# Two expert layers on one core: fetching answers in two parts, moving a branch, and roots written as powers

## The chip, the cores and the metric

The kernel runs on one core of a Trainium2 chip. A core has a matrix engine (TensorE, PE in the profile, with PEld for its weight loads), a vector engine (VectorE, DVE), a scalar engine (ScalarE, ACT), a general engine (GpSimd, POOL) and a sequencer that here only issues DMAs and branches (SyncE, SP). ACT, POOL and SP issue DMAs on their own queues. Each engine runs its instructions in order and waits on semaphores for the others.

The metric is the time of one execution on the device in microseconds (us), the median of several runs.

## The reference

The kernel computes two layers over 8 sequences of 100 tokens with 512 channels, all in float32. A context of 722 rows per sequence is attended to.

```python
x = x + cross_attention_0(layernorm(x), context)   # 16 heads of 32, causal: only the first 100 context rows count
x = x + experts_0(layernorm(x))                    # top 2 of 8 experts, 512 -> 2048 -> 512, exact gelu
x = x + cross_attention_1(layernorm(x), context)   # 16 heads of 64, keys and values of the tokens and of the 722 rows
x = x + experts_1(layernorm(x))                    # top 2 of 8 experts, 512 -> 1024 -> 512, silu gate, layernorm behind
```

In an expert layer each token goes to the two experts with the largest router logits, and its two answers are summed with softmax weights:

```python
logits = xf @ Wg.T + bg
tp, ti = top_k(softmax(logits), 2);  tp = tp / (sum(tp) + 1e-8)
x = x + tp[0] * expert[ti[0]](xf) + tp[1] * expert[ti[1]](xf)
```

Which of a token's two answers is added first makes no difference to the sum but for rounding. Each layernorm needs one over the root of a variance plus 1e-5, for every token; where two layernorms follow each other (the outer one and the block's own), the kernel takes both in one step.

## The kernel before

The 800 tokens lie in seven row tiles of 128 tokens (the last has 32). The work runs in stages, and the times below are those of the profiled execution.

- **First attention (0 to 200 us)** and its output, layernorm and router (200 to 242). `Route.group` sorts the tokens of some row tiles by expert and scatters their rows with indirect DMAs into a table `sent` in device memory (L274). `Route.order` ranks the experts by load: the fullest one gets slot 0, and so on. `values_load` (L304) brings the expert numbers of the slots into registers of SP and POOL, since they address the weights and the tables.
- **First experts (244 to 630).** `work_off` runs the eight slots one after the other. `arrived` (L351) loads a slot's rows and turns them into columns, `hidden0` does the first product (L695) with gelu on ACT, `products` the second (L363) with its bias on DVE, `returned` turns the result back and writes it with a POOL DMA (L384) to a table `answers`. The answers of slot k are written during slot k+1. Each slot has a fixed capacity (256 rows in slot 0, 176 in slot 7).
- **The branch (`rest`, L403 and L404).** If some expert has more tokens than its slot's capacity, a second round does the rest. The number `more` is loaded into registers of every engine, and every engine compares and branches. With these inputs the round is skipped. A branch also ends a block of instructions: the scheduler of the framework reorders the instructions of a block by priority and readiness, and moves none across the branch. In the kernel before it stands behind the experts.
- **Between the layers (630 to 685).** `project_early` computes five units of keys (L432, copied by ACT in L436) and values (transposes L444, copied by ACT in L446 to L449) of the second attention ahead of time. Then for each of the seven row tiles: `fetch` (L340) gathers the first answer and then the second of each token from `answers` with indirect DMAs on POOL, into a tile with two buffers; DVE adds each, scaled (L738); DVE takes mean and variance (L129, L131); `factors` makes one over the root, with ACT's Sqrt (L139) and DVE's reciprocal (L142), and the shift (L144); DVE scales (L148); PE turns the tile into columns (L159), and ACT writes these with gain and shift into `xT` (L168); POOL adds the output bias (L744). At the end the loads of the next weights start behind one-element POOL copies (L56), on SP's queue (L58).
- **Second attention (685 to 1490).** First the queries (L421). Then 64 units (sequence, pair of heads): scores (L793), row maximum on DVE (L797), exponential on ACT (L799), transposes (L822 to L828, copied by DVE and ACT), weighted values (L843). Whenever a row tile's units are done, `output` (L891) projects it, DVE adds it to x, and mean, variance and `factors` (ACT's Sqrt in L141) prepare it for the router; `logits1` (L175) and the scatter of `sent_on` follow one and two units later. Five row tiles come out inside the stage, near 924, 1015, 1139, 1328 and 1428 us, and two at its end. ACT holds the tables of one set of functions at a time: an ACT_TABLE_LOAD stands in the trace wherever an exponential follows a root or the reverse.
- **Second experts (1531 to 1831)**, another branch, and the final gathers, layernorm and output (to 1872).

The order on each engine is the framework scheduler's, block by block; DMAs are issued in the order of their queue. Weights come through a pool of eight 1 MB tiles, loaded by SP in the order of use; a load waits until the tile's last reader is done.

Of the kernel before, what the change touches and what calls it, by code (L numbers as in the profile page):

```python
# [66 lines left out]
def two_layers(ctx: ExitStack, tc: tile.TileContext, a: dict, out: bass.AP):  # L67
# [48 lines left out]
    nc.vector.memset(eps2, EPS * EPS)  # L116
    rank = const.tile([P, NE], F32, name="rank")
# [16 lines left out]
    def factors(mv, tag, twice=False):  # L134


        r = small.tile([P, 1], F32, tag=f"r{tag}", name=f"r{tag}")
        if twice:
            nc.scalar.activation(r, mv[:, 1:], AF.Sqrt, bias=eps2, scale=1.0 + EPS)  # L139
        else:  # L140
            nc.scalar.activation(r, mv[:, 1:], AF.Sqrt, bias=eps)  # L141
        nc.vector.reciprocal(r, r)  # L142
        t = small.tile([P, 1], F32, tag=f"t{tag}", name=f"t{tag}")
        nc.vector.scalar_tensor_tensor(t, mv[:, :1], -1.0, r, ALU.mult, ALU.mult)  # L144
        return r, t
# [61 lines left out]
    class Route:  # L207


        def __init__(self, layer, psum, tag):  # L210
# [6 lines left out]
            ]  # L217
            self.sel = routes.tile([P, NTILE, NE], F32, tag="sel", name=f"sel{layer}")
# [7 lines left out]
        def largest(self, v, m, name):  # L226
# [3 lines left out]
            at = self.temp([P, NTILE, NE], f"at{name}")[:, :g, :]  # L230
# [7 lines left out]
        def group(self, i0, i1, xn, held=()):  # L238
# [3 lines left out]
            at1 = self.largest(v, self.m[0][:, i0:i1], 1)  # L242
            other = self.temp([P, NTILE, NE], "other")[:, :g, :]
            nc.vector.scalar_tensor_tensor(other, at1, -3e38, v, ALU.mult, ALU.add)
            at2 = self.largest(other, self.m[1][:, i0:i1], 2)
# [17 lines left out]
            for k, at in enumerate((at1, at2)):  # L263
                pick = self.temp([P, NTILE, NE], "pick")[:, :g, :]
                nc.vector.tensor_tensor(pick, at, row, ALU.mult)
                place = self.temp([P, NTILE], "place")[:, :g]
                nc.vector.tensor_reduce(place, pick, AX.X, ALU.add)
                nc.vector.tensor_copy(self.where[k][:, i0:i1], place)
# [12 lines left out]
        def order(self, load):  # L281
# [7 lines left out]
            slot = self.temp([P, NE], "slot")  # L289
# [28 lines left out]
            nc.vector.tensor_copy(self.more, most)  # L318

# [66 lines left out]
    def work_off(jobs, arrive, hidden, product, send_back, first=None, midway=None):  # L386
# [5 lines left out]
        for k, (e, r0, n, w1, w2) in enumerate(jobs):  # L392
            h = hidden(e, n, x, w1, lambda: done and send_back(*done))
# [83 lines left out]
    with tc.tile_pool(name="a0", bufs=1) as ap, tc.tile_pool(name="a0w", bufs=3) as aw, tc.tile_pool(  # L477
# [193 lines left out]
        nc.vector.tensor_tensor(m2, m2, s, ALU.mult)  # L671


    with f0, tc.tile_pool(name="f0w", bufs=2) as fw, tc.tile_pool(
# [29 lines left out]
        def work0(jobs, first=None, midway=None):  # L704
# [3 lines left out]
                lambda e, r0, n, yT: returned(0, e, r0, n, yT, fp, ps), first, midway,  # L708
            )

        weights.limit = W_L1A + 4
# [6 lines left out]
        ], W_L0F, fetch_context)  # L718
        rest(
            more, work0, lambda piece, e, g: piece(of(0, "W1", e, g)), lambda piece, e, g: piece(of(0, "W2", e, g)), 4  # L720
        )

# [8 lines left out]
        xT1 = columns_tile("xT1")  # L731
        for i in range(NTILE):
            w = rows[i]
            both = fp.tile([P, 2, D], F32, tag="nil", name="back0", bufs=2)
            for k, m in enumerate((m1, m2)):
                y = both[:, k]
                fetch(y, where, i, k)
                nc.vector.scalar_tensor_tensor(  # L738
                    x[:w, i, :], y[:w], m[:w, i : i + 1], x[:w, i, :], ALU.mult, ALU.add
                )  # L740
            xn = fp.tile([P, D], F32, tag="mv", name="xn1", bufs=2)
            scaled(xn, x[:, i, :], *factors(moments(x[:, i, :], "a1"), "b", twice=True))
            to_columns(xT1, xn, i * P, rows[i], ps, gamma1, beta1)
            nc.gpsimd.tensor_tensor(x[:, i, :], x[:, i, :], bo, ALU.add)  # L744
        weights.limit = len(pieces)
        weights.load(W_L1A + 8, y[:1, :1])


    with tc.tile_pool(name="a1", bufs=1) as ap, ExitStack() as later, tc.tile_pool(
# [136 lines left out]
        def output(i):  # L886
# [9 lines left out]
            scaled(xn, x[:, i, :], *factors(moments(x[:, i, :], "f1"), "a"))  # L896
# [189 lines left out]
```

## Time and profile before

| | us |
|---|---|
| time before, median of 3 runs | 1872.75 (1872.5 to 1874.85) |
| profiled execution, its own time | 1873.61 |
| its span | 1872.1 |
| mean granted clock of PE | 0.962 of full speed |
| PE busy | 1730.2 (92%) |
| DVE busy | 593.0 (32%) |
| ACT busy | 482.6 (26%) |
| POOL busy | 151.6 (8%) |

The span runs from the first to the last instruction in the trace; the execution's own time is some 1.5 us longer. PE's busy share is a mean over stages. How it falls over the stages is read from windows of the trace, which give the busy time of every engine in a stretch, the clock that PE was granted there, and the share of time in which the DMA engines were busy. In a timeline of the trace each line is a group of like instructions: start, length, engine, line of the kernel, operation, what it writes and reads, and in brackets how long the engine had been idle before and which event ended that. In the list of waits a line says which tile an engine waited for, on whom, and then the sum of these waits, their number and the longest.

### The profile page before, as it was taken

The page shows a single profiled execution, that of the slowest core. Times are in us where ns is not written, and L with a number is a line of the kernel's source. Part 1 is how long each engine was busy: PE and PEld are TensorE (multiplying, and loading weights), DVE is VectorE, ACT ScalarE, POOL GpSimd, SP SyncE. Part 2 cuts the span into 40 slices and gives each one's busy share as a digit, 9 for nine tenths or more (in the row PEclk, how much of TensorE's full clock was granted, in tenths as well). Part 3 has the DMA queues.
Part 4 walks back from the last instruction along what each step waited for, and adds up shares of the span by engine and source line. Part 5 has one row for each costly group of instructions (what it writes and reads, how often), then busy time and mean ns, then how long its engine had stood idle before and what let it go on. Part 6 is the DMA issues. An engine that isn't in the chain of part 4 may idle for free. (4 is left out here: it accounts for less than half of the span.)

```text
span 1872.1 us, 26461 instructions
## 1 busy us (share of the span) xinstructions
PE 1730.2 (92%) x10422; PEld 1308.1 (70%) x10422; DVE 593.0 (32%) x1455; ACT 482.6 (26%) x1409; POOL 151.6 (8%) x245
## 2 busy tenths in 40 slices
PE   5999899999999879999999999999999839999990
PEld 2455579999999745666666666666666528999990
DVE  4464510111111130455444333444444331111115
ACT  2364321111111131333333323333333210010110
POOL 4010310000000130000000000000000030000003
PEclk9999999999999989999999999999999969999995
DMA  9911384465555371132010300211201145555513
GB/s 367 414 64 57 119 326 167 172 224 179 205 202 217 116 269 46 32 96 72 25 48 5 60 3 4 37 6 37 26 6 15 5 179 207 200 185 204 203 72 114
DMA packets 74982, 233.35 MB, mean 125 GB/s; under 512 B 23548, under 2 KB 35952, under 8 KB 58456
## 3 DMA queue, kind: packets, MB, share of 16 engines
q1 hardware_dynamic: 53348, 183.47, 28.4%
q0 software_dynamic: 9888, 30.06, 5.0%
q10 hardware_dynamic: 11604, 17.95, 3.1%
q8 instruction: 86, 1.41, 0.3%
q14 instruction: 56, 0.46, 0.1%
HBM read 180.41 MB, written 51.05 MB: 124 GB/s over the span
## 5 line engine op out<-in xcount | busy, mean ns | idle before, releaser
L432 PE MATMUL ps_m<-cb,w 128*128 128x361 f32 x896 | 302.4, 489 | 0.0
L363 PE MATMUL ps_y<-h,w 128*128 128x256 f32 (+7 forms) x1536 | 280.5, 344 | 0.0
L363 PEld LDWEIGHTS ps_y<-h,w 128*128 128x128 f32 x1536 | 268.6, 190 | 7.9
L432 PEld LDWEIGHTS ps_m<-cb,w 128*128 128x128 f32 x896 | 172.0, 197 | 103.7 <-issue 16.9
L695 PE MATMUL ps_h<-xgT,w 128*128 128x256 f32 (+7 forms) x1024 | 188.8, 345 | 0.0
L695 PEld LDWEIGHTS ps_h<-xgT,w 128*128 128x128 f32 x1024 | 180.3, 191 | 5.7 <-ACT h L699 0.2
L799 ACT ACTIVATE pr<-ps_sc,m 100x822 f32<-100x822 f32 x128 | 119.9, 942 | 176.2 <-DVE m L797 92.9
L797 DVE TENSOR_REDUCE m<-ps_sc 100x1 f32<-100x822 f32 x128 | 123.8, 1008 | 48.4 <-PE ps_sc L793 48.4
L823 DVE COPY prT<-ps_ptA 128x500 f32<-128x500 f32 x128 | 82.0, 678 | 178.2 <-PE ps_ptA L822 178.1
L699 ACT ACTIVATE h<-ps_h,s_b 128x256 f32<-128x256 f32 (+7 forms) x128 | 56.0, 438 | 303.6 <-PE ps_h L695 303.6
L436 ACT COPY mT<-ps_m 128x361 f32<-128x361 f32 x128 | 58.8, 460 | 254.7 <-PE ps_m L432 224.9
L421 PE MATMUL ps_col<-xT,w 128*128 128x400 f32 x320 | 115.0, 517 | 1.3 <-ACT xT L168 1.3
L965 PE MATMUL ps_g<-xgT,w 128*128 128x256 f32 (+7 forms) x512 | 104.0, 347 | 0.0
L965 PE MATMUL ps_u<-xgT,w 128*128 128x256 f32 (+7 forms) x512 | 102.8, 344 | 0.0
L421 PEld LDWEIGHTS ps_col<-xT,w 128*128 128x128 f32 x320 | 61.7, 196 | 47.4 <-issue 4.3
L965 PEld LDWEIGHTS ps_g<-xgT,w 128*128 128x128 f32 x512 | 91.2, 192 | 2.9
L793 PE MATMUL ps_sc<-mT,qT 64*100 64x411 f32 (+1 forms) x512 | 92.8, 468 | 0.0
L965 PEld LDWEIGHTS ps_u<-xgT,w 128*128 128x128 f32 x512 | 90.7, 190 | 2.6
L843 PEld LDWEIGHTS ps_av<-prT,mv 128*64 128x64 f32 (+1 forms) x1536 | 67.9, 137 | 27.2 <-issue 23.9
L970 ACT ACTIVATE sg<-ps_g 128x256 f32<-128x256 f32 (+7 forms) x64 | 22.3, 348 | 238.6 <-PE ps_g L965 238.6
L843 PE MATMUL ps_av<-prT,mv 128*64 128x100 f32 (+1 forms) x1536 | 80.6, 253 | 0.0
L822 PEld LDWEIGHTS ps_ptA<-ident,pr 100*128 100x128 f32 x640 | 65.3, 141 | 21.1 <-issue 11.0
(243 smaller groups left out, 1836.1 us busy)
## 6 DMA issues: line engine op xcount, KB each, us to landing
w<-in_W SPq DMA_DIRECT2D x64, 1024.0 KB
w<-in_w_gate SPq DMA_DIRECT2D x16, 1024.0 KB
w<-in_w_up SPq DMA_DIRECT2D x16, 1024.0 KB
w<-in_w_down SPq DMA_DIRECT2D x16, 1024.0 KB
sent<-nil SPq DMA_DIRECT2D x25, 512.0 KB
answers<-nil SPq DMA_DIRECT2D x25, 512.0 KB
cb<-in_ctxT ACTq DMA_DIRECT2D x16, 722.0 KB
mT<-kept_keys SPq DMA_DIRECT2D x13, 361.0 KB
```

The lines of the kernel that those rows point to most:

```text
L363: nc.tensor.matmul(py[:, k, :n], ws[f // 4][:, f % 4, dc * P : (dc + 1) * P], h[:, f, :n], start=f == 0, stop=f == nf - 1,)
L421: nc.tensor.matmul(ps[:, :HALF], w[c // 4][:, dc, (c % 4) * P : (c % 4 + 1) * P], xT[:, dc, cols], start=dc == 0, stop=dc == DC - 1,)
L432: nc.tensor.matmul(pm[:, : S // 2], w_m[ic // 4][:, dc, (ic % 4) * P : (ic % 4 + 1) * P], cb[h][:, dc, : S // 2], start=dc == 0, stop=dc = ...
L436: nc.scalar.copy(mT[:, h * (S // 2) : (h + 1) * (S // 2)], pm[:, : S // 2])
L695: nc.tensor.matmul(ph[:, :n], w[:, dc, j * P : (j + 1) * P], xg[:, dc, :n], start=dc == 0, stop=dc == DC - 1,)
L793: nc.tensor.matmul(sc[:, bank, c0:c1], qT[r, ic, q0 : q0 + T], keys_, start=True, stop=True)
L797: nc.vector.tensor_reduce(m, sc[:, :, :NKH], AX.XY, ALU.max, negate=True)
L799: nc.scalar.activation(pr.rearrange("p (a n) -> p a n", a=2), sc[:, :, :NKH], AF.Exp, bias=m, accum_out=sums[:, j : j + 1],)
L822: nc.tensor.transpose(pt[:, c, :], pr[:, T + c * P : T + (c + 1) * P], ident[:T, :T])
L823: nc.vector.tensor_copy(prT[:, : NSC - 1, :], pt)
L843: nc.tensor.matmul(po[r, 0, :], vj, prT[j][:w, c, :], start=c == 0, stop=c == NSC)
L965: nc.tensor.matmul(p_[:, :n], w_[:, dc, j * P : (j + 1) * P], xg[:, dc, :n], start=dc == 0, stop=dc == DC - 1,)
```

## The change

The diff has five parts, and `half` is a new constant tile of -0.5.

1. `rest` of the first layer moves from behind the first experts to the front of them.
2. `by_slot`, new, runs after the router: for every token it exchanges its two answers (their places in the table and their weights `m1`, `m2`) where needed, so that index 0 is the answer of the earlier slot. To that end the two one-hot choices (`at`) and the places are kept in tiles of their own. An answer of index 0 thus always comes from one of the slots 0 to 6.
3. `fetch_firsts` gathers the seven tiles of first answers while the last expert runs, behind the writing of the answers of slot 6 (`ahead` in `work_off`); they go into the buffer of `xT`, which is free then, and one into the buffer of `o_b1`. DVE adds them to x in a loop behind the experts, which the scheduler places ahead of the last expert's bias additions.
4. The second answers get one tile `seconds` with seven parts in the buffer of `h`, and their gathers are issued one after the other. The tiles `xn` have four buffers instead of two; every other row tile's columns are written by DVE instead of ACT (`vector`); the bias additions on POOL stand in a loop behind (the scheduler places them between the powers).
5. `factors(by_power=True)` makes one over the root with two POOL operations (an addition, or a multiplication and addition, and a power with exponent -0.5) in place of ACT's Sqrt and DVE's reciprocal: for the seven tiles between the layers, and for the seven outputs of the second attention. Other uses of `factors` stay.

```diff
-    def factors(mv, tag, twice=False):
+    def factors(mv, tag, twice=False, by_power=False):
         r = small.tile([P, 1], F32, tag=f"r{tag}", name=f"r{tag}")
-        if twice:
-            nc.scalar.activation(r, mv[:, 1:], AF.Sqrt, bias=eps2, scale=1.0 + EPS)
+        if by_power:
+            if twice:
+                nc.gpsimd.tensor_scalar(r, mv[:, 1:], 1.0 + EPS, EPS * EPS, ALU.mult, ALU.add)
+                nc.gpsimd.tensor_tensor(r, r, half, ALU.pow)
+            else:
+                nc.gpsimd.tensor_scalar(r, mv[:, 1:], EPS, None, ALU.add)
+                nc.gpsimd.tensor_tensor(r, r, half, ALU.pow)
         else:
-            nc.scalar.activation(r, mv[:, 1:], AF.Sqrt, bias=eps)
-        nc.vector.reciprocal(r, r)
+            ...
+            nc.vector.reciprocal(r, r)
...
+        def by_slot(self, behind):
+            wide = self.temp([P, NTILE, NE], "pick")
+            nc.gpsimd.tensor_copy(wide[:1, 0, :1], behind[:1, :1])
+            slots = [self.temp([P, NTILE], t) for t in ("key", "mine")]
+            for at, t in zip(self.at, slots):
+                nc.vector.tensor_tensor(wide, at, self.slot.unsqueeze(1).to_broadcast([P, NTILE, NE]), ALU.mult)
+                nc.vector.tensor_reduce(t, wide, AX.X, ALU.add)
+            swap = slots[0]
+            nc.vector.tensor_tensor(swap, slots[0], slots[1], ALU.is_gt)
+            for pair in (self.places, self.m):
+                d = slots[1]
+                nc.vector.tensor_tensor(d, pair[1], pair[0], ALU.subtract)
+                nc.vector.tensor_tensor(d, d, swap, ALU.mult)
+                other = self.temp([P, NTILE], "first")
+                nc.vector.tensor_tensor(other, pair[1], d, ALU.subtract)
+                nc.vector.tensor_tensor(pair[0], pair[0], d, ALU.add)
+                nc.vector.tensor_copy(pair[1], other)
+            for k in range(2):
+                nc.vector.tensor_copy(self.where[k], self.places[k])
...
-    def work_off(jobs, arrive, hidden, product, send_back, first=None, midway=None):
+    def work_off(jobs, arrive, hidden, product, send_back, first=None, midway=None, ahead=None):
...
-            h = hidden(e, n, x, w1, lambda: done and send_back(*done))
+            last = k + 1 == len(jobs)
+            h = hidden(e, n, x, w1, lambda: (done and send_back(*done), last and ahead and ahead()))
...
+        route.by_slot(where[1])
...
+        firsts = turned_x.tile([P, NTILE - 1, D], F32, tag="xT", name="firsts")
+        firsts = [firsts[:, i] for i in range(NTILE - 1)]
+        SHORT_AT = rows.index(min(rows))
+        firsts.insert(SHORT_AT, fp.tile([P, D], F32, tag="o_b1", name="first_short"))
+        def fetch_firsts():
+            for i in range(NTILE):
+                fetch(firsts[i], where, i, 0)
+        rest(more, work0, ...)
         weights.limit = W_L1A + 4
         work0([
             ...
-        ], W_L0F, fetch_context)
-        rest(more, work0, ...)
+        ], W_L0F, fetch_context, fetch_firsts)
+        for i, w in enumerate(rows):
+            nc.vector.scalar_tensor_tensor(
+                x[:w, i, :], firsts[i][:w], m1[:w, i : i + 1], x[:w, i, :], ALU.mult, ALU.add
+            )
...
+        seconds = fw.tile([P, NTILE, D], F32, tag="h", name="seconds", bufs=1)
+        for i in range(NTILE):
+            fetch(seconds[:, i], where, i, 1)
         for i in range(NTILE):
             w = rows[i]
-            both = fp.tile([P, 2, D], F32, tag="nil", name="back0", bufs=2)
-            for k, m in enumerate((m1, m2)):
-                y = both[:, k]
-                fetch(y, where, i, k)
-                nc.vector.scalar_tensor_tensor(
-                    x[:w, i, :], y[:w], m[:w, i : i + 1], x[:w, i, :], ALU.mult, ALU.add
-                )
-            xn = fp.tile([P, D], F32, tag="mv", name="xn1", bufs=2)
-            scaled(xn, x[:, i, :], *factors(moments(x[:, i, :], "a1"), "b", twice=True))
-            to_columns(xT1, xn, i * P, rows[i], ps, gamma1, beta1)
+            nc.vector.scalar_tensor_tensor(
+                x[:w, i, :], seconds[:w, i, :], m2[:w, i : i + 1], x[:w, i, :], ALU.mult, ALU.add
+            )
+            xn = fp.tile([P, D], F32, tag=("mv", "nil")[i % 2], name="xn1", bufs=2)
+            scaled(xn, x[:, i, :], *factors(moments(x[:, i, :], "a1"), "b", twice=True, by_power=True))
+            to_columns(xT1, xn, i * P, rows[i], ps, gamma1, beta1, vector=i % 2 == 1)
+        for i in range(NTILE):
             nc.gpsimd.tensor_tensor(x[:, i, :], x[:, i, :], bo, ALU.add)
         weights.limit = len(pieces)
-        weights.load(W_L1A + 8, y[:1, :1])
+        weights.load(W_L1A + 8, seconds[:1, NTILE - 1, :1])
...
-            scaled(xn, x[:, i, :], *factors(moments(x[:, i, :], "f1"), "a"))
+            scaled(xn, x[:, i, :], *factors(moments(x[:, i, :], "f1"), "a", by_power=True))
```

## The prediction

> **What bounds the kernel now.** I read the stages first (busy time of each engine in eight stretches), since one share of busy time hides them.
>
> ```profile
> 244.00:630.00 386.00, 384.65 (x2167) 372.20 (x2168) 40.59 (x108) 57.31 (x129) 16.95 (x36) 1.00 0.55 201
> 630.00:685.00 55.00, 37.95 (x149) 23.78 (x147) 26.71 (x53) 21.69 (x61) 25.15 (x27) 0.86 0.61 211
> 685.00:1490.00 805.00, 788.45 (x5157) 504.39 (x5158) 321.10 (x656) 265.17 (x734) 16.81 (x34) 0.98 0.17 36
> ```
>
> The columns are length, busy PE, PEld, DVE, ACT, POOL, granted clock, DMA share, GB/s. PE fills the first experts (384.65 of 386 us) and nearly fills the second attention (788.45 of 805). Only the stretch between the layers has idle PE worth a name, 17 us. So three places can answer the change: that stretch, PE's few pauses in the attention, and the start of the experts, where the branch goes.
>
> Between the layers I read the timeline of POOL, DVE, ACT and PE. Lines are start, length, engine, operation, and in brackets the idle time before and its releaser.
>
> ```profile
> 642.39 1.05 POOL L340 DMA_INDIRECT back<-answers,where  x1 [5.91 <-ACT mv L449]
> 664.57 1.14 POOL L340 DMA_INDIRECT back<-answers,where  x1 [0.30 <-issue]
> 646.81 1.54 DVE L738 SCALAR_TENSOR_TENSOR x<-back,m,x 128x512 f32<-128x512 f32 x2 [13.88 <-DMA back<-answers,where]
> 649.85 0.29 ACT L139 ACTIVATE rb<-mv_a,eps 128x1 f32<-128x1 f32 x1 [4.95 <-DVE mv_a L131]
> 678.42 0.16 DVE L142 RECIPROCAL rb<-rb 128x1 f32<-128x1 f32 x1 [5.15 <-ACT rb L139]
> 682.52 0.55 DVE L148 TENSOR_SCALAR xn<-x,rb,tb 128x512 f32<-128x512 f32 x1
> 685.09 5.61 PE L421 MATMUL ps_col<-xT,w 128*128 128x400 f32 x8 [1.27 <-ACT xT L168]
> ```
>
> Fourteen gathers run from 642.39 to 665.7; then ACT is the bottleneck: it does the root (L139) and the eviction (L168) in one queue, and DVE stands 5.15 us for a root. The last xn ends at 683.07, the projection starts at 685.09. PE's own waits there:
>
> ```profile
> PE ps_mv L444 <- ACT mT L436: 8.3, 5, 4.6
> PE ps_tp L159 <- DVE tb L144: 3.4, 1, 3.4
> ```
>
> The 4.6 is ACT standing at the root (649.85) with the keys' eviction behind it.
>
> In the attention I looked where an output tile (L891) is followed by its root, at the second of five places:
>
> ```profile
> 1013.78 1.28 ACT L799 ACT_TABLE_LOAD   x1 [3.01 <-issue]
> ...
> 1016.16 0.41 PE L793 MATMUL ps_sc<-kT,qT 64*100 64x100 f32 x2 [1.55 <-ACT pr L799]
> 1017.09 0.41 PE L793 MATMUL ps_sc<-kT,qT 64*100 64x100 f32 x2 [0.51 <-ACT pr L799]
> 1017.71 1.48 PE L175 MATMUL ps_lg<-p_w_router,xTf 128*128 128x8 f32 x8 [0.20 <-ACT xTf L161]
> 1019.04 8.05 PE L432 MATMUL ps_m<-cb,w 128*128 128x361 f32 x16
> ```
>
> The exponential reloads its table after the root, PE waits 2.06 us, and then 16 matmuls that elsewhere take 5.03 us take 8.05. The granted clock in short steps shows why (the first two steps are from the first layer's router, for comparison):
>
> ```profile
> 214.00:217.00 3.00, 1.56 (x12) 1.28 (x13) 2.49 (x18) 1.91 (x6) 0.00 (x0) 1.00 0.30 90
> 220.00:223.00 3.00, 0.56 (x1) 0.50 (x2) 2.65 (x22) 1.18 (x3) 1.91 (x2) 0.50 0.56 216
> ...
> 1015.00:1020.00 5.00, 3.12 (x14) 2.52 (x15) 1.06 (x6) 2.64 (x7) 0.00 (x0) 0.82 0.02 0
> 1020.00:1025.00 5.00, 5.00 (x9) 2.81 (x9) 1.91 (x12) 0.46 (x1) 0.00 (x0) 0.50 0.07 3
> 1025.00:1030.00 5.00, 5.00 (x35) 3.45 (x33) 2.36 (x5) 1.22 (x5) 0.00 (x0) 1.00 0.05 8
> ```
>
> **Attention (before 1490): roots as powers.** Two POOL operations replace ACT's root (0.29 us) and DVE's reciprocal (0.16) per output; with no root, both table loads per output go. Five outputs (around 924, 1015, 1139, 1328, 1428) lie inside the stage. PE's waits there are 1.33 + 4 x 2.06 = 9.6 us. Without the 1.28 us load before the exponential, each first wait (1.33 or 1.55) shrinks by that: 5 x 1.28 = 6.4 us. The clock: the following projection's matmuls cost 2.6, 3.0, 2.4, 1.8 and 1.5 us more than at full clock (0.314 us each), 11.3; the router's eight tiny matmuls before them up to 0.8 more than their 1.06, 2.2 in sum: 13.5 us. Does the clock come back with the waits? In the first layer's router, with the same tiny matmuls but pauses of at most 1.05 us, the clock holds 1.00; the pause of 3.11 us at 219.3 to 222.4 halves it. 0.27 + 0.51 us would remain, nearer to the first case, so I let four of five falls go: 10.8. Sum -17; ends -6.4 (only waits) and -20. The cover for the power: mv_f is ready at 914.26 and DVE's next copy that PE needs (prT, behind the scaling in DVE's queue) starts at 917.92, so 3.7 us are free. ACT loses work here and nobody waits for it more.
>
> The skill ("TensorE: Matmul & The Clock Gate", Part 1) says the gate halves the clock after at least one idle window of about 3.4 us. Taken strictly, pauses of 2.06 us would not halve it, the fall would have another cause, and the attention's gain would be 6.4, the sum about 1857. The trace shows the clock at 0.50 right behind such a pause, so I keep the rows' figure.
>
> **Price of the power.** No such operation is in the trace. Nearest POOL rows: a 1x1 copy 0.17, a 100x128 copy 0.29, a 128x512 addition 1.26. The operand is 128x1, so I take 0.3 for each of the two operations, ends 0.17 and 1.26.
>
> **Between the layers.** First answers: seven gathers (0.97 us + 0.30 issue, from the rows above 1.27 each) go behind expert 6's answers, which landed at 603.89 and 608.53. So they run from about 609 to 618, with x += of 7 x 0.75 us on DVE to about 623. The bias evictions of the last expert stand behind them on DVE; the first product pair is done at 620.8 and the other PSUM half is free, so PE waits for nothing. Cover gone: at most 2 us.
>
> Second answers start when the last expert's answers have landed (640.92 before). The branch was not their bound on POOL: its reset step waited for that same landing. So about 642, and with no buffer to wait for, 7 x 1.27 to 650.9. DVE sees the first one at about 646 (landing took 4.4 us in the first row). Then per tile x += 0.75, statistics 0.69 + 0.17, t 0.15, scaling 0.53: 2.29, seven tiles 16.0; four DVE evictions of tile 1 at 0.33 in between, 1.3; five of POOL's bias additions collide (one such collision stretched two x += from 1.5 to 3.08, so 0.75 each), 3.75; the last tile's trip to POOL behind one bias addition, about 2. The last xn ends at 646 + 16.0 + 1.3 + 3.75 + 2 = 669; eight DVE evictions of 0.33 and an ACT eviction follow, the projection starts at about 672.5 to 673. Against 685.09 that is -12. PE's early keys no longer bind: five units at 5.51 (the unstalled period at 231 to 236) from 630.6 to 661 after losing their stop behind the root. Ends: if the branch's absence on DVE lets the last answers be written 2.7 us earlier (POOL waited "[2.78 <-DVEq L404]" at 635.95), and the power is cheapest, -16. If each POOL operation costs 1.26, POOL does 7 x 2.5 + five additions of 1.26 + 0.5 of copies from 652 on, and ps_col starts at about 680: -5. The Wkv pieces come earlier; PE did not wait for them.
>
> **The branch in front.** After the layer PE lost nothing to it: its branch took 3.42 us at 631.84 while matmuls already queued ran on. In front PE has nothing queued. Last transposes end at 242.1, register load 0.75 (SP's row), branch 3.42: 246.3, against 244.44 for the first transposes of the gathered rows: +1.9. At ACT's and SP's 5.4 us for the branch, +3.8. If PE's branch is hidden after all, the rows' load remains: POOL's reset waits for the sends' landing (238.03, as the load's own wait does), then about 1.4 us to the next issue as at 641, where 0.7 stood: +0.8. I take +2. (The skill, "Advanced Engine Details and Errata", Control Flow Timing, prices a compare-and-branch at about 108 ns; by it the front would cost the +0.8 alone and the sum be about 1846. The branches of this trace took 2.9 to 5.4 us.) SP's seven weight loads move from 244.56 to some 250; the third piece is needed at 261.4: hidden, at most 5 us left of cover. DVE's by_slot (17 operations, 0.17 to 0.3 each, some 4 us) waits for the sends (238.03) to rewrite the places, then the branch of 2.9, to about 243, before the rows land at 244.3: hidden. The seven expert numbers loaded together on POOL (0.6 each) run in its wait of 10.0 us.
>
> **The last two outputs (1488, 1503)** lie on a bare chain: 0.45 us of root and reciprocal become two POOL operations, +0.15 each, with queue hops +0.25: +0.5; ends -0.2 and +4.
>
> **Sum.** -12 - 17 + 2 + 0.5 = -26.5 against the profiled execution's 1873.61 (span 1872.1 and 1.5 outside) gives 1847.1; the median of the three runs lies 0.86 below the profiled one, so 1846.2; I say 1847.
>
> **Rivals.** (A) Only the waits go, the clock falls as before, because the tiny matmuls after the output do it. For: it falls right at them. Against: the first layer's router. Attention -6.4 instead of -17: 1857. (B) The stretch between the layers is held by the answers' landing and by POOL's single queue, now with roots and additions: -5 there: 1853; together with A 1864. (C) The other side: the power is slow on POOL. With p us for a pair, the projection starts at 652 + 7p + 6.8 + 3.5; at p = 3.3 nothing is won between the layers, and from p = 3.7 each output also holds DVE's prT copy, and so PE. The total is 7(p - 3.3) + 5(p - 3.7) - 17 + 2.5; it turns slower at p = 4.7, and p = 6 gives +16: 1889. For: no row. Against: every POOL row of this size is under 0.3 us. (D) The change doesn't do what it says: the first gathers land too late, or x += waits on DVE into the last expert and holds its evictions. The landing at 608.53 and the 12 us to 620.8 speak against it; -4 in all there: 1854.
>
> **How the numbers follow.** Forecast 0.52, A 0.20, B 0.10, C 0.12, D 0.04, something near no change 0.02. Below 0.2% (3.7 us) a measurement of this kernel cannot tell from no change. Faster: forecast, A, B and D, less a little, 0.85; same 0.03; slower 0.12. The range runs from all good ends (-16 - 20 + 0.8 = -35.2: 1837) to A with B (1864). C stays out above it.
>
> **What would show it.** Right: no ACT_TABLE_LOAD and no wait over 0.6 us at the five outputs, 16 matmuls of L432 after them in about 5 us, first gathers before 620, the projection's first matmul some 42 us behind the end of the last product (630.2 before) instead of 55, the first ps_h 2 us later. Wrong: POOL rows of the power over 1.3 us; DVE idle "<-POOL r"; a clock of 0.5 at 1020 still; PE waiting for weights at the start of the experts; a branch of over 5 us on PE.

## The result and the profile after

The changed kernel takes 1858.86 us (median of 5 runs, 1856.08 to 1864.6) against 1874.85 us for the kernel before (5 runs): the ratio is 0.9921, with a 95% interval of 0.9896 to 0.9947. It is faster by 0.8%, about 16 us, where 26 had been forecast. The profiled execution is the slowest of the five (1864.6 us, span 1863.1); so the stages below say where time went, and the medians how much. All line numbers of the changed kernel differ from those of the kernel before (the products L695 are L732, the keys L432 are L468, the exponential L799 is L850, the gathers L340 are L375).

Cut at five marks of PE (end of the last value transposes before the experts, start of the first product, end of the last product, start of the projection, start of the last output's matmuls), the spans of the two profiles are, in us:

| stage | before | after |
|---|---|---|
| last transposes to first product of the experts | 5.3 | 11.6 |
| first experts, first to last product | 382.9 | 383.7 |
| last product to the projection | 54.8 | 45.3 |
| projection to the last output of the attention | 808.1 | 798.8 |
| the rest | 379.0 | 378.9 |

So the gain of 9.4 us between the layers and of 9.3 in the attention stands against a loss of 6.3 in front. (A further 2.7 us of this profile were lost earlier, in the router, where the clock fell 2.9 us sooner, at 216.59 instead of 219.45, around the same matmuls, and stayed low twice as long.)

The front, by the timeline of PE and POOL of the changed kernel (start, length, engine, operation, idle before and its releaser). The last line but one is PE's two branches (ns min/median/max, first and last start), and the last line is the same load in the kernel before:

```profile
244.11 0.66 PE L480 MATMUL ps_mv<-ident,mT 128*128 128x128 f32 x4 [0.33 <-ACT mT L472]
253.09 1.94 PE L169 MATMUL ps_tp<-ident,xg 128*128 128x128 f32 x8 [8.32 <-DMA xg<-sent]
256.38 5.89 PE L732 MATMUL ps_h<-xgT,w 128*128 128x256 f32 x16
249.40 1.18 POOL L386 DMA_DIRECT2D xg<-sent  x2 [15.74 <-PEq L440]
L440 PEldq COMPARE_BRANCH  x2: 3562/3915/4268, 244.7 to 1816.6; - x2
238.71 1.19 POOL L351 DMA_DIRECT2D xg<-sent  x2 [6.56 <-PE ps_m L432]
```

PE stands 8.32 us for the rows of the first expert. POOL had done its own part of the branch at 241.5, with the rows scattered (landed at 239.9); the load was issued at 249.40, and what released it is PE's sequencer at the branch (L440): PE's record of the branch lasts 4.27 us, to 249.0. The first rows landed at 252.95, and only then could PE transpose.

Between the layers (POOL, DVE, PE):

```profile
619.17 1.05 POOL L375 DMA_INDIRECT firsts<-answers,where  x1 [3.80 <-ACT h L736]
631.11 0.73 DVE L770 SCALAR_TENSOR_TENSOR x<-first_short,m,x 32x512 f32<-32x512 f32 x1
645.35 0.56 POOL L419 DMA_DIRECT2D answers<-y  x1 [2.39 <-DMA answers<-y]
648.41 1.01 POOL L375 DMA_INDIRECT seconds<-answers,where  x1 [2.50 <-ACT mv L485]
656.07 1.23 POOL L375 DMA_INDIRECT seconds<-answers,where  x1 [0.30 <-issue]
663.42 0.16 DVE L154 SCALAR_TENSOR_TENSOR tb<-mv_a,rb 128x1 f32<-128x1 f32 x1 [3.14 <-POOL rb L143]
679.03 0.55 DVE L158 TENSOR_SCALAR xn<-x,rb,tb 128x512 f32<-128x512 f32 x1
685.39 7.08 PE L457 MATMUL ps_col<-xT,w 128*128 128x400 f32 x12 [1.28 <-ACT xT L178]
```

Everything lies 9.7 us later than in the kernel before, since the experts ended at 640.08 instead of 630.34. The first answers are gathered and added under the last expert. The seven second gathers take 648.41 to 657.3; then the chain of DVE and POOL sets the end, with DVE idle for powers (the line at 663.42; in all 6.9 us over seven tiles).

The second attention at the same output as shown before:

```profile
1012.15 0.41 PE L844 MATMUL ps_sc<-kT,qT 64*100 64x100 f32 x2 [0.27 <-ACT pr L850]
1013.08 0.41 PE L844 MATMUL ps_sc<-kT,qT 64*100 64x100 f32 x2 [0.51 <-ACT pr L850]
1013.70 1.06 PE L185 MATMUL ps_lg<-p_w_router,xTf 128*128 128x8 f32 x8 [0.21 <-ACT xTf L171]
1014.61 6.80 PE L468 MATMUL ps_m<-cb,w 128*128 128x361 f32 x16
...
1423.58 5.11 PE L468 MATMUL ps_m<-cb,w 128*128 128x361 f32 x16
```

The wait of 1.55 us is 0.27, which is what the table load of 1.28 leaves. But the 16 matmuls behind still take 6.80 us here, 5.11 at the last of the five outputs. The windows of the trace (length, PE, PEld, DVE, ACT, POOL, clock, DMA share, GB/s) show the same two cases:

```profile
1010.00:1015.00 5.00, 4.01 (x46) 3.20 (x45) 2.46 (x6) 2.58 (x6) 0.00 (x0) 1.00 0.02 0
1015.00:1020.00 5.00, 5.00 (x12) 2.94 (x11) 2.40 (x14) 0.46 (x1) 0.00 (x0) 0.66 0.00 0
1418.00:1423.00 5.00, 4.01 (x45) 2.65 (x42) 2.56 (x6) 2.58 (x6) 0.00 (x0) 1.00 0.01 3
1423.00:1428.00 5.00, 5.00 (x22) 3.40 (x22) 2.31 (x14) 0.46 (x1) 0.00 (x0) 1.00 0.02 0
```

PE is busy for the same 4.01 of 5 us ahead of both, and once the clock falls (a mean of 0.66 over the next 5 us) and once it stays.

### The profile page after: what moved, and what is told of

It reads as the page before. It is cut to its first block, busy times and chain, and to the rows that moved or that the text cites. A ratio compares the mean times of both kernels' runs of the same rounds, so it can differ in the third digit from the quotient of the medians.

```text
span 1863.1 us, 26486 instructions
## 1 busy us (share of the span) xinstructions
PE 1729.1 (93%) x10422; PEld 1308.5 (70%) x10422; DVE 595.6 (32%) x1471; ACT 458.5 (25%) x1370; POOL 164.7 (9%) x274
## 5 line engine op out<-in xcount | busy, mean ns | idle before, releaser
L468 PE MATMUL ps_m<-cb,w 128*128 128x361 f32 x896 | 298.1, 483 | 0.0
L468 PEld LDWEIGHTS ps_m<-cb,w 128*128 128x128 f32 x896 | 169.7, 195 | 102.1 <-issue 13.9
L732 PE MATMUL ps_h<-xgT,w 128*128 128x256 f32 (+7 forms) x1024 | 189.7, 346 | 0.0
L732 PEld LDWEIGHTS ps_h<-xgT,w 128*128 128x128 f32 x1024 | 180.9, 192 | 5.8
L850 ACT ACTIVATE pr<-ps_sc,m 100x822 f32<-100x822 f32 x128 | 120.0, 942 | 188.8 <-DVE m L848 95.8
L844 PE MATMUL ps_sc<-mT,qT 64*100 64x311 f32 (+1 forms) x512 | 92.1, 468 | 0.0
L873 PEld LDWEIGHTS ps_ptA<-ident,pr 100*128 100x128 f32 x640 | 65.3, 141 | 20.7 <-issue 10.5
```

The source lines that it names most:

```text
L468: nc.tensor.matmul(pm[:, : S // 2], w_m[ic // 4][:, dc, (ic % 4) * P : (ic % 4 + 1) * P], cb[h][:, dc, : S // 2], start=dc == 0, stop=dc = ...
L732: nc.tensor.matmul(ph[:, :n], w[:, dc, j * P : (j + 1) * P], xg[:, dc, :n], start=dc == 0, stop=dc == DC - 1,)
L844: nc.tensor.matmul(sc[:, bank, c0:c1], qT[r, ic, q0 : q0 + T], keys_, start=True, stop=True)
L850: nc.scalar.activation(pr.rearrange("p (a n) -> p a n", a=2), sc[:, :, :NKH], AF.Exp, bias=m, accum_out=sums[:, j : j + 1],)
L873: nc.tensor.transpose(pt[:, c, :], pr[:, T + c * P : T + (c + 1) * P], ident[:T, :T])
```

## The experiments

Three theories stood after the first look. Front: the branch delays the load of the first rows, against chance and the vector work of `by_slot`. Attention: the clock falls on account of the tiny router matmuls (or of their position), against the waits alone. Between the layers: the early gathers carry the gain, against powers, buffers and shared evictions. In what follows a "fall" is an output at which the granted clock drops to half during PE's waits, the router's matmuls or the matmuls of L468 behind them. "Excess" is what the router's eight matmuls and those of L468 took, at the five outputs, over their time at full clock (1.06 us for the eight, 1.16 when wide; 0.3145 each of L468), summed.

### The changed kernel again, and the branch alone

> The changed kernel unaltered, run beside the others so that they have a neighbour on the same chip. Expected 1856 to 1864 us, 10 to 18 below the kernel before. In its first profile the first product of the first experts began 9.0 us later than before (256.38 against 247.43) and the second attention took 9.3 us less. If the late start is the branch, it comes back here within 2 us (252 to 258); if it was the chance position of a clock fall in the router, it is at 250 or below.

Measured: 1859.79 us (6 runs) against 1872.58 before, ratio 0.9928 (0.9904 to 0.9951). Last transposes to first product 11.3 us: the late start is no chance. Falls at all five outputs, excess 12.2 us (four and 10.6 in the first profile).

```diff
--- the kernel before
+++ front_branch
+        rest(more, work0, ..., 4)
         weights.limit = W_L1A + 4
         work0([...], W_L0F, fetch_context)
-        rest(more, work0, ..., 4)
```

> The kernel before with only the branch moved in front of the first experts. Theory 1: the first ps_h at about 254 (247.4 plus the register load, the branch of 3.4 to 4.3 us and a DMA of 3.6 us that no longer runs beside them, less 2.3 us that PE waited for the rows anyway): +6 us there; behind the experts PE's branch was hidden before, so little comes back, 0 to 2; total +4 to +7 us against before. My recorded price of +2 would give +0 to +2. Theory 2: 0 within 2 us.

Measured: 1879.37 us, ratio 1.0036 (1.0024 to 1.0047), 6.8 us slower. Last transposes to first product 11.5 instead of 5.3 us. POOL's line shows the same releaser:

```profile
251.09 1.94 PE L159 MATMUL ps_tp<-ident,xg 128*128 128x128 f32 x8 [8.20 <-DMA xg<-sent]
247.45 1.18 POOL L351 DMA_DIRECT2D xg<-sent  x2 [15.99 <-PEq L404]
```

This kernel has neither `by_slot` nor powers, so the branch alone costs the 6 us, and taking it away behind the experts gives nothing back there: the stretch from the last product to the projection is 54.4 us (54.8 before). In the kernel before, the timeline of PE says why: two matmuls of the early keys stand ahead of the last transposes, and the rest of that unit follows ahead of PE's branch, so PE had work while it branched. (The description of the kernel said that nothing is moved across a branch. The first unit of the early keys was.)

```profile
630.61 0.77 PE L432 MATMUL ps_m<-cb,w 128*128 128x361 f32 x2
631.22 0.60 PE L381 MATMUL ps_yt<-ident,yT 128*128 128x128 f32 x4
631.65 4.42 PE L432 MATMUL ps_m<-cb,w 128*128 128x361 f32 x14
```

### The branch back behind the experts

```diff
--- the changed kernel
+++ late_branch
-        rest(more, work0, ..., 4)
         weights.limit = W_L1A + 4
         work0([...], W_L0F, fetch_context, fetch_firsts)
+        rest(more, work0, ..., 4)
```

> The changed kernel with the branch back behind the first experts, the first answers still gathered ahead. It leaves one thing out: if the second round were ever taken, its first answers would be missed; with these inputs it is skipped. Theory 1 (the branch in front costs 6 to 9 us, since POOL's load of the first rows waits until PE has passed its branch, and only then does the DMA run): the first ps_h comes back to 246 to 250, and between the layers POOL's second gathers start about 3 us later relative to the last product (as the 12.1 us from the last product to the first gather before, against 8.3 after); the sum is 3 to 6 us below the changed kernel of this call. Theory 2 (the late start is chance or by_slot's vector work): the first ps_h stays at 252 or later, and the sum is equal to the changed kernel or up to 4 us above it.

Measured: 1849.27 us (6 runs, 1847.09 to 1857.08), ratio 0.9887 (0.9867 to 0.9907), 10.5 below the changed kernel of the same call. Stage by stage: 5.8 us in front (11.3), 48.9 from the last product to the projection (44.6), so 1.3 us net from the branch (2.2 against the other profile of the changed kernel). The first gather of the second answers begins 12.6 us behind the last product instead of 8.3. The rest of the difference, 10.3 us in the profiles, lies in the attention (789.7 against 800.1), whose instructions are the same in both: one fall instead of five, excess 2.2 instead of 12.2. So theory 1 holds for the front, but the branch is worth only about 2 us net. In the two profiles the rest is the clock's (10.0 of the 10.3).

The same output, with the same waits and no fall:

```profile
1003.59 0.41 PE L844 MATMUL ps_sc<-kT,qT 64*100 64x100 f32 x2 [0.27 <-ACT pr L850]
1004.52 0.41 PE L844 MATMUL ps_sc<-kT,qT 64*100 64x100 f32 x2 [0.51 <-ACT pr L850]
1005.14 1.06 PE L185 MATMUL ps_lg<-p_w_router,xTf 128*128 128x8 f32 x8 [0.21 <-ACT xTf L171]
1006.05 5.11 PE L468 MATMUL ps_m<-cb,w 128*128 128x361 f32 x16
```

### The powers in the attention alone

```diff
--- the kernel before
+++ powers_attention
-            scaled(xn, x[:, i, :], *factors(moments(x[:, i, :], "f1"), "a"))
+            scaled(xn, x[:, i, :], *factors(moments(x[:, i, :], "f1"), "a", by_power=True))
```

> The kernel before with powers in place of roots in the second attention alone. Theory A (only the waits of the table loads go, 6.4 us; the clock still falls behind most outputs, by the router's tiny matmuls): 6 to 10 us below before, falls at three or more of the five outputs. Theory of the prediction (waits and clock falls both go): 16 to 18 below, falls at one output at most. If the gain of the attention came from the other parts (other alignment): within 2 us of before.

Measured: 1860.69 us, ratio 0.9938 (0.9918 to 0.9958), 11.9 us below before. PE's waits for the exponential are 3.1 us in all, where they were 9.6. Falls at five of five outputs in its profile, which is again its slowest run (1868.59, the others 1854.86 to 1866.25). The attention's part of the change is this one edit, and its size lies between the two theories, nearer to A: 6.5 us of waits, and about 5 of excess by the means of the table further down.

### What makes the clock fall

```diff
--- the changed kernel
+++ wide_logits
-            router_logits(route.logits, i, xTf, wg1, None, ps, "tp")
+            pl = ps.tile([P, 16, NE], F32, tag="tp", name="ps_lg")
+            for dc in range(DC):
+                nc.tensor.matmul(pl[:w], xTf[:, dc, :w], wg1[:, dc, :].unsqueeze(1).to_broadcast([P, 16, NE]),
+                                 start=dc == 0, stop=dc == DC - 1)
+            nc.vector.tensor_copy(route.logits[:w, i, :], pl[:w, 0, :])
```

> The changed kernel with the second attention's router matmuls 128 columns wide instead of 8 (the same 8 columns of weights read 16 times; only the first 8 results are used). PE's waits before them stay as they are (0.99 us in four of five outputs). Theory 1 (a stretch in which PE is idle or does tiny matmuls, 2 us in all, still makes the clock fall if it meets the gate's period badly; 15 of 20 outputs in the four profiles with powers): the wide matmuls count as work, falls at no more than one of five outputs, the excess of the following projections sinks from 9 to 11 us to under 3, the wider matmuls cost about 0.6 to 1.1 us per output in seven outputs; total 2 to 6 us below the changed kernel (ratio to before 0.989 to 0.992). Theory 2 (PE's waits alone make the clock fall): three or more falls stay, total 4 to 8 us above the changed kernel (ratio 0.994 to 0.998).

Measured: 1854.72 us (1853.05 to 1857.9), ratio 0.9916 (0.9903 to 0.993). The waits are unchanged. The excess is 3.5 us with two falls, one more than theory 1 allowed; this is the second output, which has none:

```profile
1007.10 0.41 PE L844 MATMUL ps_sc<-kT,qT 64*100 64x100 f32 x2 [0.51 <-ACT pr L850]
1007.72 1.16 PE L940 MATMUL ps_lg<-p_w_router,xTf 128*128 128x128 f32 x8 [0.21 <-ACT xTf L171]
1008.72 5.03 PE L468 MATMUL ps_m<-cb,w 128*128 128x361 f32 x16
```

Matmuls sixteen times as wide cost 0.10 us for all eight (1.16 against 1.06). The whole kernel is 4 to 5 us below the changed one by the medians, which come from different calls, but only 1 to 2 us by the ratios to the kernel before of each call, whose intervals overlap. So a gain in total time is not shown by this run.

The same edit to the kernel before (its waits of 2.06 us stay):

> The kernel before with the wide router matmuls alone; the waits of 2.06 us for the table load stay. If the tiny matmuls are what makes a stretch too idle for the clock, falls go from five of five to two or fewer, and it is 5 to 10 us below before. If waits of 2 us alone suffice, falls stay at four or five, and it is 0 to 3 us below. Together with powers_attention this says how much of the prediction's 10.8 us of clock belongs to the waits.

Measured: 1868.63 us, ratio 0.9976 (0.9966 to 0.9987), 3.5 us below before. The excess is 6.2 us, with three falls; two of them began in the waits themselves, 0.9 and 0.5 us ahead of the router's matmuls. So the waits alone still make the clock fall at some outputs. Neither of the two pure theories holds. All profiles together:

| kernels | profiles | falls of outputs | excess per profile, us |
|---|---|---|---|
| roots (waits 2.06), narrow matmuls | 2 | 9 of 10 | 12.5 |
| powers (waits 0.78), narrow | 8 | 25 of 40 | 7.4 (2.2 to 12.2) |
| roots, wide | 1 | 3 of 5 | 6.2 |
| powers, wide | 3 | 4 of 15 | 2.3 (0.1 to 3.5) |

(The eight are the profiles of the changed kernel, its repetition, late_branch, powers_attention, root_between, xg_ahead, xg_ahead_root and no_ahead: 4, 5, 1, 5, 3, 5, 1 and 1 falls.)

Identical instructions fall at one output and not at the next, and the traces show why: it is their position in time. Within each of the fourteen traces, all drops of the granted clock begin a whole number of steps of 3.413 us apart, to 0.003 us. In the changed kernel's trace the falls at 926.57, 1015.31, 1134.78 and 1322.51 are 26, 35 and 55 steps apart. Call these points marks. Windows cut at the marks (columns as before), for the second and the fifth output:

```profile
1011.90:1015.31 3.41, 2.44 (x15) 1.89 (x16) 0.85 (x5) 1.74 (x6) 0.00 (x0) 1.00 0.03 0
1015.31:1018.73 3.42, 3.42 (x7) 1.98 (x6) 2.12 (x13) 0.00 (x0) 0.00 (x0) 0.50 0.00 0
1421.50:1424.91 3.41, 2.69 (x16) 2.04 (x16) 1.37 (x8) 1.11 (x4) 0.00 (x0) 1.00 0.03 0
1424.91:1428.32 3.41, 3.41 (x13) 2.15 (x12) 1.34 (x9) 0.46 (x1) 0.00 (x0) 1.00 0.00 0
```

Falls at outputs 2 to 5 of all profiles (the first output has another order), by how far behind the last mark the router's matmuls begin; the bounds of the rows are read from the cases themselves:

| behind the mark, us | powers, narrow | powers, wide | roots, narrow | roots, wide |
|---|---|---|---|---|
| 0.17 to 1.17 | 0 of 10 | 0 of 6 | 3 of 3 | 2 of 2 |
| 1.21 to 2.60 | 12 of 12 | 0 of 2 | 2 of 2 | 0 of 1 |
| 2.69 to 3.29 | 8 of 8 | 4 of 4 | 3 of 3 | 1 of 1 |
| 3.35 to 3.36 | 0 of 2 | - | - | - |

So with powers and narrow matmuls the position alone separates all 32 cases. At like positions the longer waits add falls (first row), and so do the tiny matmuls (second row, where the wide cases are few). How much idle time within a step is enough was not worked out. No run set the position on purpose: the first mark lies 0.28 to 3.26 us behind the start of a trace, and so the same instructions gave five falls in one profile and one in another.

### Between the layers

```diff
--- the changed kernel
+++ no_ahead
-        ], W_L0F, fetch_context, fetch_firsts)
+        ], W_L0F, fetch_context)
+        fetch_firsts()
```

> The changed kernel with all fourteen gathers behind the last expert: seven first answers and seven second ones back to back, each into a buffer of its own. If the early gathers carry the gain between the layers (forecast: seven gathers of 1.27 us less in front of the chain), the stretch from the last product to the projection grows from 45 to 50 to 54 us, total 5 to 9 us above the changed kernel. If the gain there came from the seven buffers, from DVE writing every other tile and from the roots off ACT's queue, and the gathers are hidden behind PE's early keys (29 us), it grows by 0 to 3.

Measured: 1863.87 us, ratio 0.9959 (0.9944 to 0.9975). The stretch from the last product to the projection is 53.8 us, against 45.3 with the early gathers and 54.8 before.

```profile
693.89 6.58 PE L457 MATMUL ps_col<-xT,w 128*128 128x400 f32 x13 [1.28 <-ACT xT L178]
```

The seven gathers of 1.27 us, 8.9 in all, are worth 8.5. What else the change does in this stretch (seven buffers, DVE writing every other tile, roots off ACT) gives 1 us together, when all gathers stand behind the last expert.

```diff
--- the changed kernel
+++ root_between
-            scaled(xn, x[:, i, :], *factors(moments(x[:, i, :], "a1"), "b", twice=True, by_power=True))
+            scaled(xn, x[:, i, :], *factors(moments(x[:, i, :], "a1"), "b", twice=True))
```

> The changed kernel with ACT's root and DVE's reciprocal back between the layers, powers only in the second attention. Theory 1 (POOL's queue, powers behind bias additions of 1.26 us and behind the weights' copies, is what holds the stretch: DVE stood 3.1, 1.1 and five times 0.4 to 0.7 us for a power, about 7 in all; ACT has room since it writes only every other tile): the stretch from the last product to the projection falls from 45.3 to 40 to 44 us, total 1 to 5 us below the changed kernel. Theory of the prediction (the powers are what frees the stretch, since ACT's root in its queue was the bottleneck before): 47 to 52 us, total 2 to 6 above.

Measured: 1855.76 us, ratio 0.9931 (0.9912 to 0.9951); the stretch is 44.2 us (45.3 and 44.6 with powers). The waits for powers go, and others take their place:

```profile
659.69 0.29 ACT L149 ACTIVATE rb<-mv_a,eps 128x1 f32<-128x1 f32 x1 [1.20 <-DVE mv_a L133]
670.02 0.55 DVE L158 TENSOR_SCALAR xn<-x,rb,tb 128x512 f32<-128x512 f32 x1 [2.70 <-PE ps_tp L169]
680.90 9.53 PE L457 MATMUL ps_col<-xT,w 128*128 128x400 f32 x19 [2.51 <-ACT xT L178]
```

Here the kind of root makes no difference that can be measured; both theories were too bold.

### Loading rows ahead of the branch

```diff
--- the changed kernel
+++ xg_ahead
+        xg0 = turned_x.tile([P, CAP // P, D], F32, tag="xT", name="xg_first")
+        for s in range(CAP // P):
+            nc.gpsimd.dma_start(out=xg0[:, s, :], in_=rows_of(sent, 0, 0, s * P, P))
         rest(more, work0, ..., 4)
```

The tile takes the place of `xg` for the first expert; `firsts` takes over its buffer later.

> The changed kernel with the first expert's rows loaded ahead of the branch (into the buffer of xT), the branch still in front. If the load waits for PE's branch and its 3.6 us lie bare behind it, the first ps_h begins about 3 to 4 us earlier relative to the end of the values' transposes (8 to 9 us instead of 11.3 to 11.6), total 3 to 4 below the changed kernel; PE's own branch of 4.3 us stays. If PE's branch alone sets the start and the load is not what it waits for, 0 within 1.

Measured: 1863.09 us, ratio 0.9962 (0.995 to 0.9975): slower than the changed kernel, by 3 to 4 us by the medians and 6 to 8 by the ratios. The wait had only moved:

```profile
246.44 1.94 PE L169 MATMUL ps_tp<-ident,xg_first 128*128 128x128 f32 x8 [4.63 <-PEq L444]
259.67 0.88 PE L169 MATMUL ps_tp<-ident,xg 128*128 128x128 f32 x3 [11.29 <-DMA xg<-sent]
260.34 5.16 PE L736 MATMUL ps_h<-xgT,w 128*128 128x256 f32 x16
252.50 1.20 POOL L390 DMA_DIRECT2D xg<-sent  x2 [7.53 <-issue]
```

The first transposes come as soon as PE has branched. But PE's order puts three transposes of the second expert ahead of the first product, and those rows now come later: POOL branched only after it had waited for the first rows and loaded its registers, and issued them at 252.5.

> Both edits of the two kernels before together (rows loaded ahead of the branch; root and reciprocal back between the layers). They lie in different stages, so their differences to the changed kernel should add: with theory 1 for each, 4 to 8 us below the changed kernel, ratio to before about 0.989; with the prediction's theory for the root, about equal to it.

Measured: 1864.74 us, ratio 0.9976 (0.9958 to 0.9993), the same wait (18.0 us from the last transposes to the first product): nothing gained from the second edit.

So the rows of both experts were loaded ahead, together with the wide matmuls:

```diff
--- xg_ahead
+++ xg2_wide (and wide_logits' edit)
+        xg_first = turned_x.tile([P, 2, CAP // P, D], F32, tag="xT", name="xg_first")
+        for e in range(2):
+            for s in range(CAP // P):
+                w = min(P, CAPS[e] - s * P)
+                nc.gpsimd.dma_start(out=xg_first[:w, e, s, :], in_=rows_of(sent, 0, e, s * P, w))
```

> The changed kernel with the rows of the first two experts loaded ahead of the branch, and the wide router matmuls. With one expert's rows ahead, the first transposes began 4.6 us after the values' transposes instead of 8.3, but PE then stood 11.3 us for the second expert's rows, which the order of PE puts ahead of the first product. If that is the whole of its loss, the first ps_h now begins 7 to 8 us after the values' transposes (11.3 to 11.6 in the changed kernel) and the total is 3 to 4 us below the wide kernel: 1849 to 1852, ratio to before 0.988 to 0.990. If loading ahead costs for another reason (POOL's branch later, weights later), the first ps_h is at 11 us or more.

Measured: 1851.46 us (5 runs, 1847.59 to 1853.83) against 1872.1, ratio 0.9887 (0.987 to 0.9903). First product 8.0 us after the last transposes:

```profile
249.60 1.94 PE L169 MATMUL ps_tp<-ident,xg_first 128*128 128x128 f32 x8 [4.72 <-PEq L444]
252.20 0.90 PE L169 MATMUL ps_tp<-ident,xg_first 128*128 128x128 f32 x3 [0.67 <-DVE xgT L176]
252.90 6.00 PE L736 MATMUL ps_h<-xgT,w 128*128 128x256 f32 x16
```

> The same with root and reciprocal back between the layers. root_between shortened the stretch from the last product to the projection by 0.4 to 1.1 us: expected 0 to 1 us below xg2_wide, which a measurement will hardly tell. If the powers between the layers matter, 2 us or more above.

Measured: 1850.17 us, ratio 0.9887 (0.9872 to 0.9903): no difference from xg2_wide. Both are 7 to 10 us below the changed kernel's medians (6 to 8 by the ratios), and the best of the kernels here that keep the second round complete. What is left in front is mainly PE's own branch, the 4.7 us of the first line.

## Why the prediction was right, and where it was not

The direction and the range held: 1858.86 lies within 1837 to 1864. The forecast of 1847 was 12 us too good. Its terms against what the runs showed, in us:

| term | forecast | measured |
|---|---|---|
| attention, waits of the table loads | -6.4 | -6.5 (9.6 to 3.1) |
| attention, clock falls | -10.8 | -5.1 (excess 12.5 to 7.4 per profile, means of the table) |
| between the layers | -12 | -9.4 and -10.1 (the two profiles) |
| branch in front | +2 | +6.0 to +6.3 |
| last two outputs | +0.5 | +0.9 (PE's two waits for xnf: 3.03 to 3.48 and 3.39 to 3.82) |
| sum | -26.5 (with 17.2 of the attention taken as 17) | about -14 (medians: -13 and -16) |

Rival A's 1857 lies nearer to 1858.86 than the forecast does, but partly by luck: its error in the clock (0 instead of -5.1) is outweighed by those of the other terms (about +6.6 together).

**Waits of the table loads.** Right to 0.1 us, place by place: without the load the first wait falls from 1.55 to 0.27. The cover was right too: a pair of POOL operations took 0.28 + 0.58 = 0.86 us on average between the layers (0.6 assumed, 2.5 the bound), and PE shows no wait for a copy behind a power in the attention.

**Clock falls.** This was the term that was most mis-sized. The step that failed is "nearer to the first case, so I let four of five falls go". It compared 0.78 us of waits with the pauses of the first layer's router, where the clock had held, as if a fall were decided by the length of the waits. That case was itself a matter of position: in the changed kernel's trace the clock fell at 216.59, behind the same pause of 1.05 us and at the same router matmuls of the first layer. Rival A came true for the larger part: with the waits cut, 25 of 40 falls stayed, and position decided which. The router's tiny matmuls count as near-idle time and add to the waits: at positions where the narrow ones fell, the wide ones held. The Trainium skill's page "TensorE: Matmul & The Clock Gate" (Part 1) says that the activity window is free-running and that its effect varies from run to run. The traces agree, with the marks every 3.413 us and their different place against each start. The page's rule of at least one idle window of about 3.4 us does not fit as it stands: the clock fell at 1015.31 behind a step in which PE was busy for 2.44 of 3.41 us.

**Branch in front.** Two steps failed. The smaller is PE's branch, 4.27 us instead of 3.42. The larger: I let the load of the rows run beside PE's branch ("if PE's branch is hidden after all, the rows' load remains", +0.8), so that the longer of two paths counted. In fact the load was issued only when PE had passed its branch, so that branch, DMA and transposes stand in a row. In the kernel before the same load waited for a matmul of PE (released at 238.49 by L432); that the framework turns such a wait into one for PE's passing, where a branch lies between, is read from the releaser, in two kernels. The bound of +3.8 was therefore too low. The skill's page "Advanced Engine Details and Errata" (Control Flow Timing) has some 108 ns for a compare-and-branch; PE's record in this profile has 4.27 us.

**Between the layers.** The mechanism was right, and no_ahead shows that the gathers carry it (8.5 of 9.4). The early gathers and their additions came where forecast, 9.7 us later with everything else: the gathers from 619.2 (609 forecast), the additions to 631.8 (623). Two errors of opposite sign nearly cancel. The second gathers began 8.3 us behind the last product, not 12. I had written that the branch was not their bound on POOL, since its reset step waited for the same landing; but the last write was issued 5.3 us behind the last product (5.6 before), landed 2.3 us later, and the gathers followed. With the branch there (before and late_branch) they began after 12.1 and 12.6, so it was a bound, of about 4 us. And the chain behind took 27 us instead of 23 (from 652.39 to 679.58), since DVE stood 6.9 us for powers behind POOL's other work. The powers themselves were neither the gain nor the loss there.

**Rival B** (the answers' landing and POOL's queue hold the stretch to -5) is out in its size, since the stretch gave -9.4 and -10.1, though POOL's queue did hold DVE for 6.9 us. **Rival C** (a slow power) is out: no power between the layers took over 0.73 us. **Rival D** is out: the first gathers had landed in time.

What stays open: late_branch is some 10 us below the changed kernel by the medians, of which the branch explains 2. Its profile has one fall, since outputs 2 to 4 lay 0.48 to 0.86 us behind a mark. It is not that one run alone: its six runs have a mean granted clock of 0.967, the changed kernel's six of the same call 0.962. Whether its runs had luck with the marks, or whether a kernel's timing from its start puts it at a better position, was not tried.

## What to carry to other kernels

A branch costs not only the engine that waits for it but every load that depends on another engine's earlier work: issue the loads of the first work behind the branch ahead of it, for all the tiles that the next engine touches before its first real matmul. Gathers that can be started under the previous stage are worth their issue time, one for one, when they lead the chain. Where PE runs long at full clock with short pauses, count tiny matmuls as pauses; widening them costs little and leaves fewer positions at which the clock falls. Do not judge such a stage by one profile: the same instructions gave one to five falls.

## What the runs showed of the hardware

- The clock falls behind 2 us of waits and tiny matmuls at 25 of 40 places with identical instructions. The falls of a trace begin on marks 3.413 us apart, and the position against them decides (all 32 cases of outputs 2 to 5). The clock stays at 0.50 for one or two such steps, and with powers a fall costs the router's matmuls and those behind them 1.7 to 1.9 or 3.4 us.
- Eight float32 matmuls with 128 moving columns take 1.16 us where eight with 8 columns take 1.06.
- A power with exponent -0.5 of 128x1 took POOL 0.55 to 0.58 us alone, the operation before it 0.19 to 0.25.
- A branch took PE 4.27 us in front of the experts and 3.42 behind them, and DVE about 3.
